# The router's product with its weights stationary, and the logits transposed back one step later, in a two-layer graph attention and mixture-of-experts kernel

## The chip, the cores and the metric

The kernel runs on one core of one Trainium2 chip. The core has five engines that run at the same time, each through its own list of instructions in order: TensorE (PE, matrix products and transposes, writing to PSUM), VectorE (DVE), ScalarE (ACT), GpSimd (POOL) and SyncE (SP, which here starts most of the transfers). They wait for each other through semaphores. The metric is the time of the whole kernel on the device in microseconds, the median over several runs.

## What is computed

The input is 128 graphs of 64 nodes with 256 features each, which makes 8192 rows (tokens). Two layers follow each other. Each adds to `x` first a graph attention of the normalised `x`, and then a mixture of experts of the normalised result. This change concerns the router of the mixture of experts, which picks two of eight experts for each row. Cut down to it:

```python
# layer 0
logits = tokens @ router_w.T                  # (8192, 256) @ (256, 8)
probs = softmax(logits); rw, re = top_k(probs, 2); rw = rw / rw.sum()
out = tokens + sum_e combine[:, e] * (gelu(tokens @ w1[e] + b1[e]) @ w2[e] + b2[e])
# layer 1
logits = x @ Wg + bg + bias                   # (8192, 256) @ (256, 8)
vals, idx = top_k(logits, 2); w = softmax(vals)
out = sum_e combine[:, e] * (relu(x @ W1[e] + b1[e]) @ W2[e] + b2[e])
```

All arithmetic is in 32-bit floating point.

## The kernel before

The rows are worked in blocks of 512 (four tiles of 128), 16 blocks in each layer, so 32 blocks. For each block there are two Python generators: `attend` (the attention) and `route` (layer norm, router, the places of the rows in the experts' lists). Each `yield` ends a step. Beside them, `Slots` works through the experts' lists in slots of 256 rows: `x` fetches the rows' transposes (px, L764; xT, L768), `h` makes the first product (ph, L846) with its activation (hT, L855), and `y` makes the second product (py, L877) and adds its bias (ys, L884). Layer 0 then scatters the rows by an indirect transfer (L893); layer 1 first weights them (L919) and adds them to the output (L922).

The order of the work is written out by hand: a loop over the blocks calls one step of one generator after the other. PE, DVE, ACT and SP run their instructions in exactly that order. POOL is not in that list, and its order is left to the framework's scheduler. For the block `t` that is being routed and the next one `n = t + 1` in attention, the part of the loop that matters here reads, before the change:

```python
a(n)          # pe (L309, L310), ee, the maximum (L325), the exponentials (L328)
r(t)          # pl (L419), lg, largest, the write of xb (L439)
if t + 2 != NB:
    a(t + 2)  # layer 1 only: eight DVE additions to xs (L267)
y()           # py (L877), ys (L884)
a(n)          # 1/sum (erc, L334) and its product with ee (L335)
(h if more else x)()
r(t)          # the second largest logit
a(n)          # pp: transposes of ee (L339), and their copies (L341, L342)
y()
```

The router's product itself has the transposed rows of the block as its stationary operand, and 8 columns of weights stream through: `pl[:, t, :]` (128 rows by 8 logits) is made by two products for each of the four tiles. DVE copies `pl` to `lg` (L428, or L430 and L431 with the biases in layer 1), and `largest` finds the largest logit, its place and its one-hot row (L372 to L383). The first three blocks run through chains that are written out beforehand, in which the steps of several blocks alternate; `(r, 0)] * 10` is the number of steps of such a chain.

PSUM tiles of the router share a ring of two buffers (tag `r`): two for the transposes of the rows (pt), one for pl, one for pn (L476). Tiles of one tag in SBUF share a ring too: tag `ex` has three buffers, and each block of the attention uses two.

Of the kernel before, what the change touches and what calls it, by code (L numbers as in the profile page):

```python
# [8 lines left out]
F32 = mybir.dt.float32  # L9
# [7 lines left out]
P = 128  # L17
NG = 64
D = 256
KD = D // P  # L20
E = 8
TT = 4
TB = TT * P
# [12 lines left out]
def adj_ffn_kernel(  # L36
# [34 lines left out]
    nc = tc.nc  # L71
# [19 lines left out]
    work = ctx.enter_context(tc.tile_pool(name="work", bufs=3))  # L91
    small = ctx.enter_context(tc.tile_pool(name="small", bufs=2))
    slot = ctx.enter_context(tc.tile_pool(name="slot", bufs=2))
    ps_c = ctx.enter_context(tc.tile_pool(name="ps_c", bufs=2, space=bass.MemoryType.PSUM))
# [25 lines left out]
    ident = const.tile([P, P], F32, name="ident")  # L120
# [5 lines left out]
    for g in range(2):  # L126
        r = slice(g * NG, (g + 1) * NG)
# [10 lines left out]
    start = const.tile([P, E], F32, name="start")  # L138
# [48 lines left out]
    rw = [const.tile([P, KD, E], F32, name=f"rw{l}") for l in range(2)]  # L187
# [57 lines left out]
    def transposed(src, tag, ptag, name, both):  # L245

        xt = work.tile([P, KD, TB], F32, tag=tag, name=f"xt_{name}", bufs=2)
        for k in range(KD):
            pt = ps_c.tile([P, TB], F32, tag=ptag, name=f"pt_{name}_{k}")
            for t in range(TT):  # L250
                nc.tensor.transpose(
                    pt[:, t * P : (t + 1) * P], src[:, t, k * P : (k + 1) * P], ident
                )
            if k % 2 == 0 and not both:
                nc.vector.tensor_copy(xt[:, k, :], pt)  # L255
            else:
                nc.scalar.copy(xt[:, k, :], pt)
        return xt
# [136 lines left out]
    def unordered(group, ins, keep=()):  # L395

        tc.declare_no_dep(
            ins.ins, group=group, keep=[i.ins for i in keep], reason="different rows"
        )
        tc.add_to_no_dep_group(group, ins.ins)  # L400

    def route(l, b, blk):

        name = f"r{l}_{b}"
# [8 lines left out]
        yield  # L413
        tT = transposed(tn, "tT", "r", name, l == 0 and b < FIRST)
        yield
        pl = ps_c.tile([P, TT, E], F32, tag="r", name=f"pl_{name}")
        for t in range(TT):
            for k in range(KD):
                nc.tensor.matmul(  # L419
                    pl[:, t, :],  # L420
                    lhsT=tT[:, k, t * P : (t + 1) * P],
                    rhs=rw[l][:, k, :],
                    start=(k == 0),
                    stop=(k == KD - 1),
                )
        lg = small.tile([P, TT, E], F32, tag="lg", name=f"lg_{name}")
        if l == 0:
            nc.vector.tensor_copy(lg, pl)  # L428
# [27 lines left out]
        r = slice(b * TT, (b + 1) * TT)  # L456
# [232 lines left out]
    class Slots:  # L689
# [139 lines left out]
        def h(self):  # L829
            k = self.nh  # L830
            self.weighted()
            if k == self.nx or k == self.ny + 2:
                return
            self.nh += 1
            sl = self.all[k]
            l = sl["l"]
            wc, xT = sl["wc"], sl["xT"]
            hT = slot.tile([P, HC[l], SL], F32, tag="hT", name=f"hT_s{k}")
            for f in range(0, HC[l], 2):
                ph = ps_s.tile([P, 2, SL], F32, tag="ph", name=f"ph_s{k}_{f}", bufs=2)  # L840
                cols = [slice(r.start * P, r.stop * P) for _, r in sl["of"]]
                for j in range(2):
                    for w, r in zip(wc, cols):
                        for c in range(KD):
                            o = c * HC[l] * P + (f + j) * P
                            nc.tensor.matmul(  # L846
                                ph[:, j, r],
                                lhsT=w[:, o : o + P],
                                rhs=xT[:, c, r],
                                start=(c == 0),  # L850
                                stop=(c == KD - 1),
                            )
                for j in range(2):
                    for w, r in zip(wc, cols):
                        nc.scalar.activation(  # L855
                            hT[:, f + j, r], ph[:, j, r], AF.Gelu if l == 0 else AF.Relu,
                            bias=w[:, OB1[l] + f + j : OB1[l] + f + j + 1],
                        )
            sl["hT"] = hT
            if l == 1 and sl["rest"]:  # L860
                self.spare(k)

        def y(self):
            k = self.ny
            self.weighted()
            if k == self.nh:
                return
            self.ny += 1
            sl = self.all[k]
            l = sl["l"]  # L870
            wc, hT = sl["wc"], sl["hT"]
            py = ps_s.tile([P, ST, D], F32, tag="py", name=f"py_s{k}")
            ys = slot.tile([P, ST, D], F32, tag="ys", name=f"ys_s{k}", bufs=4)
            for w, (_, r) in zip(wc, sl["of"]):
                for t in range(r.start, r.stop):
                    for f in range(HC[l]):
                        nc.tensor.matmul(  # L877
                            py[:, t, :],
                            lhsT=hT[:, f, t * P : (t + 1) * P],
                            rhs=w[:, O2[l] + f * D : O2[l] + (f + 1) * D],  # L880
                            start=(f == 0),
                            stop=(f == HC[l] - 1),
                        )
                nc.vector.tensor_tensor(  # L884
                    ys[:, r, :],
                    py[:, r, :],
                    w[:, OB2[l] : OB1[l]].unsqueeze(1).to_broadcast([P, r.stop - r.start, D]),
                    ALU.add,
                )
            sl["ys"] = ys  # L890
            for t in range(sl["st"]):
                if l == 0:
                    ins = nc.gpsimd.indirect_dma_start(  # L893
                        out=res[sl["part"]],
                        out_offset=self.row(sl, t),
                        in_=ys[:, t, :],
                        in_offset=None,
                        bounds_check=2 * N - 1,
                        oob_is_err=False,
                    )  # L900
                    unordered(f"res{sl['part']}", ins)
            if l == 1:
                self.ready = k
            self.ahead()
# [59 lines left out]
    def there(i):  # L964
        return 0 <= i < len(blks) and blks[i]

    def load(i, first=None):
        if there(i):
            k = blks[i]
            if k["l"]:  # L970
                assert all(s["l"] or s["part"] != part(k["b"]) for s in slots.all[slots.ny :])
            k["in"] = load_block(k["l"], k["b"], first)
            k["a"] = attend(k["l"], k["b"], k)

    def a(i, n=1):
        if there(i):
            for _ in range(n):
                next(blks[i]["a"], None)

    def r(i, n=1):  # L980
        if there(i):
            k = blks[i]
            if "r" not in k:
                k["r"] = route(k["l"], k["b"], k)
            for _ in range(n):
                next(k["r"], None)
# [15 lines left out]
    place = counted("place", [P, ST], [[P, ST]], 0, 1)  # L1002
    att = lambda b: [(a, b)] * 9 + [(a, b, 2), (a, b)]
    chains = [
        (0, att(0)[3:] + [(r, 0)] * 10),
        (1, att(1)[2:] + [(r, 1)] * 10),
        (2, att(2) + [(r, 2)] * 9),
        (8, att(3) + [(r, 3)] * 2),
        (12, [(a, 4)] * 3),
    ]  # L1010
# [28 lines left out]
    for t in range(FIRST, len(blks)):  # L1039
        n = t + 1  # L1040
        more = slots.nf - slots.ny > SB or len(slots.all) - slots.ny > SB
        if t + 3 != NB:
            load(t + 3)
        a(n)
        h()
        x()
        a(n)
        r(t - 1)
        a(n)
        h()  # L1050
        r(t)
        slots.fetch()
        if more:
            x()
        a(n)
        r(t)
        if t + 2 != NB:
            a(t + 2)
        y()
        a(n)  # L1060
        (h if more else x)()
        r(t)
        a(n)
        y()
        a(t + 2, 1 + (t + 2 == NB))
        if more:
            x()
        a(n)
        r(t)
        h()  # L1070
        a(n)
        if more:
            y()
        x()
        a(n)
        h()
        r(n)
        y()
        a(t + 2)
        r(t)  # L1080
        r(t)
        y()
        slots.fetch()
        x()
        r(n)
        r(t)
        if t + 3 == NB:
            load(t + 3)
# [57 lines left out]
```

## Time and profile before

| | before |
|---|---|
| median of 3 runs | 1437.01 us (1436.83 to 1442.47) |
| the profiled execution, its own time | 1675.06 us |
| span of the profile, first to last instruction | 1673.3 us |
| mean granted clock of TensorE | 0.882 of full |
| L419, the router's product, PE | 512 records, 81.8 us busy |
| L877 and L846, the experts' products, PE | 425.6 and 402.1 us busy |

The profile is one execution, taken by the hardware profiler, and it took longer than the runs without it. An engine's busy time is the time in which it had an instruction at work; the two rows of products are pipelined, so their records overlap, and the distance from one start to the next says more than the length of one. A product in 32-bit floating point appears as two records (two passes). In brackets a line of a timeline gives the idle time of the engine just before an instruction, and what ended it.

### The profile page before, as it was taken

The page shows a single profiled execution, that of the slowest core. Times are in us where ns is not written, and L with a number is a line of the kernel's source. Part 1 is how long each engine was busy: PE and PEld are TensorE (multiplying, and loading weights), DVE is VectorE, ACT ScalarE, POOL GpSimd, SP SyncE. Part 2 cuts the span into 40 slices and gives each one's busy share as a digit, 9 for nine tenths or more (in the row PEclk, how much of TensorE's full clock was granted, in tenths as well). Part 3 has the DMA queues.
Part 4 walks back from the last instruction along what each step waited for, and adds up shares of the span by engine and source line. Part 5 has one row for each costly group of instructions (what it writes and reads, how often), then busy time and mean ns, then how long its engine had stood idle before and what let it go on. Part 6 is the DMA issues. An engine that isn't in the chain of part 4 may idle for free. (4 is left out here: it accounts for less than half of the span.)

```text
span 1673.3 us, 22326 instructions
## 1 busy us (share of the span) xinstructions
PE 1305.4 (78%) x6240; PEld 1100.9 (66%) x6240; DVE 875.1 (52%) x3390; ACT 647.5 (39%) x1550; POOL 743.9 (44%) x729
## 2 busy tenths in 40 slices
PE   7657777777777667766768888988888988869994
PEld 5546665655665556555657777877777777658883
DVE  4555755574455566745565555655555654442331
ACT  5534444444433434333333434333344434223331
POOL 3164444444445543334442455444455444544324
PEclk9668988998888898788789999988889888989997
DMA  6535555575565654656765768666777656677873
GB/s 194 143 124 176 197 167 168 167 219 167 167 184 189 228 186 152 204 171 198 219 219 156 218 194 234 197 169 193 208 215 213 172 134 185 169 218 223 238 211 65
DMA packets 262829, 311.69 MB, mean 186 GB/s; under 512 B 40615, under 2 KB 219950, under 8 KB 262704
## 3 DMA queue, kind: packets, MB, share of 16 engines
q1 hardware_dynamic: 219552, 225.02, 43.7%
q0 software_dynamic: 43152, 85.24, 19.1%
q8 instruction: 50, 0.82, 0.2%
q14 instruction: 75, 0.61, 0.1%
HBM read 212.25 MB, written 99.75 MB: 186 GB/s over the span
## 5 line engine op out<-in xcount | busy, mean ns | idle before, releaser
L846 PE MATMUL ph_s<-xT_s,wc_s 128*128 128x256 f32 (+1 forms) x1760 | 402.1, 380 | 57.3 <-DVE xT_s L768 22.8
L877 PE MATMUL py_s<-wc_s,hT_s 128*128 128x256 f32 x1648 | 425.6, 411 | 21.8 <-issue 14.0
L846 PEld LDWEIGHTS ph_s<-xT_s,wc_s 128*128 128x128 f32 x1760 | 327.0, 198 | 116.3 <-DVE xT_s L768 29.9
L877 PEld LDWEIGHTS py_s<-wc_s,hT_s 128*128 128x128 f32 x1648 | 331.7, 207 | 75.9 <-issue 16.6
L922 POOL DMA_INDIRECT out_dram<-ys_s,to_s x135 | 212.8, 1576 | 366.7 <-ACT ys_s L919 215.7
L499 POOL DMA_INDIRECT lists<-tn_r,ix_r x256 | 249.5, 975 | 102.9 <-issue 71.9
L855 ACT ACTIVATE hT_s<-ph_s,wc_s 128x256 f32<-128x256 f32 (+1 forms) x440 | 175.8, 457 | 278.5 <-issue 117.2
L290 PE MATMUL pw_g<-gw,xt_g 128*128 128x258 f32 x512 | 157.6, 459 | 134.0 <-ACT wh_g L297 74.0
L893 POOL DMA_INDIRECT res<-ys_s,to_s x142 | 146.2, 1029 | 259.7 <-DVE erc_g L334 177.9
L290 PEld LDWEIGHTS pw_g<-gw,xt_g 128*128 128x128 f32 x512 | 109.5, 228 | 169.5 <-ACT wh_g L297 83.3
L768 DVE COPY xT_s<-px_s 128x512 f32<-128x512 f32 (+1 forms) x140 | 95.5, 682 | 204.4 <-remote 89.4
L884 DVE TENSOR_TENSOR ys_s<-py_s,wc_s 128x512 f32<-128x512 f32 (+1 forms) x149 | 97.4, 654 | 188.6 <-PE py_s L877 180.7
L419 PE MATMUL pl_r<-rw,xt_r 128*128 128x8 f32 x512 | 81.8, 295 | 45.4 <-DVE xt_r L255 40.9
L419 PEld LDWEIGHTS pl_r<-rw,xt_r 128*128 128x128 f32 x512 | 82.1, 246 | 51.7 <-DVE xt_r L255 45.2
L297 ACT COPY wh_g<-pw_g 128x258 f32<-128x258 f32 x128 | 47.0, 375 | 162.4 <-remote 82.0
L919 ACT ACTIVATE ys_s<-ys_s,cf_s 128x256 f32<-128x256 f32 x135 | 61.4, 500 | 105.7 <-DVE ys_s L884 105.4
L240 ACT ACTIVATE tn_r<-xb_g,nb_r,rs_r 128x256 f32<-128x256 f32 x128 | 66.5, 590 | 86.3 <-DVE nb_r L238 55.5
L240 ACT ACTIVATE xn_g<-xs,nb_g,rs_g 128x256 f32<-128x256 f32 x128 | 66.4, 590 | 66.3 <-DVE nb_g L238 66.3
L764 PE MATMUL px_s<-ident,xg_s 128*128 128x128 f32 x554 | 85.7, 278 | 0.2 <-DMA xg_s<-lists 0.2
L764 PEld LDWEIGHTS px_s<-ident,xg_s 128*128 128x128 f32 x554 | 70.7, 146 | 13.0 <-issue 1.0
L348 PE MATMUL po_g<-wh_g,pT_bd 128*128 128x256 f32 x256 | 70.8, 425 | 8.5 <-ACT pT_bd L342 7.0
L342 ACT COPY pT_bd<-pp_g 64x256 f32<-64x256 f32 x32 | 11.7, 365 | 163.7 <-DVE pT_bd L341 160.6
(503 smaller groups left out, 1583.8 us busy)
## 6 DMA issues: line engine op xcount, KB each, us to landing
wc_s<-in_w_dram SPq DMA_DIRECT2D x142, 512.0 KB
wc_s<-in_w_dram SPq DMA_DIRECT2D x156, 256.0 KB
xg_s<-lists SPq DMA_DIRECT2D x64, 260.0 KB
xg_s<-lists SPq DMA_DIRECT2D x64, 258.0 KB
yb<-res SPq DMA_DIRECT2D x16, 1024.0 KB
wc_s<-bcat SPq DMA_DIRECT2D x78, 129.0 KB
wc_s<-bcat SPq DMA_DIRECT2D x71, 130.0 KB
xs<-in_x_dram SPq DMA_DIRECT2D x16, 512.0 KB
```

What stands on the lines that cost most here:

```text
L240: nc.scalar.activation(outs(t), xb[:, t, :], AF.Identity, bias=nb[:, t : t + 1], scale=rs[:, t : t + 1])
L290: nc.tensor.matmul(pw, lhsT=xt[:, k, t * P : (t + 1) * P], rhs=gw[l][:, k, :], start=(k == 0), stop=(k == KD - 1),)
L419: nc.tensor.matmul(pl[:, t, :], lhsT=tT[:, k, t * P : (t + 1) * P], rhs=rw[l][:, k, :], start=(k == 0), stop=(k == KD - 1),)
L499: ins = nc.gpsimd.indirect_dma_start(out=lists[l], out_offset=bass.IndirectOffsetOnAxis(ap=ix[:, k, t : t + 1], axis=0), in_=tn[:, t, 0 : ...
L764: nc.tensor.transpose(px[:, c, t * P : (t + 1) * P], xg[:, t, c * P : (c + 1) * P], ident)
L768: nc.vector.tensor_copy(xT[:, :, 0 : st * P], px[:, :, 0 : st * P])
L846: nc.tensor.matmul(ph[:, j, r], lhsT=w[:, o : o + P], rhs=xT[:, c, r], start=(c == 0), stop=(c == KD - 1),)
L855: nc.scalar.activation(hT[:, f + j, r], ph[:, j, r], AF.Gelu if l == 0 else AF.Relu, bias=w[:, OB1[l] + f + j : OB1[l] + f + j + 1],)
L877: nc.tensor.matmul(py[:, t, :], lhsT=hT[:, f, t * P : (t + 1) * P], rhs=w[:, O2[l] + f * D : O2[l] + (f + 1) * D], start=(f == 0), stop=(f ...
L884: nc.vector.tensor_tensor(ys[:, r, :], py[:, r, :], w[:, OB2[l] : OB1[l]].unsqueeze(1).to_broadcast([P, r.stop - r.start, D]), ALU.add,)
L893: ins = nc.gpsimd.indirect_dma_start(out=res[sl["part"]], out_offset=self.row(sl, t), in_=ys[:, t, :], in_offset=None, bounds_check=2 * N - 1,
L922: ins = nc.gpsimd.indirect_dma_start(out=out, out_offset=self.row(sl, t), in_=ys[:, t, :], in_offset=None, compute_op=ALU.add,)
```

## The change

The two operands of the router's product change sides. The weights (128 by 8) become the stationary operand, and the 512 rows of the block stream through in one product for each half of the features: 2 products instead of 8. The result `pq` stands the other way round, 8 logits by 512 rows. ACT copies it to SBUF (`lT`, in a buffer of tag `ex`), and there the step ends. A new step transposes it back on PE, four transposes of 8 by 128, into `pl` as it was. From there on nothing is different.

In the loop, the first of the two steps stands where the old one stood, and the second stands behind `y()`. So in the order of the engines `py` and `ys` come ahead of the transposes and of `lg` and `largest`, and so do the additions to `xs` of layer 1. The chains of the first blocks get one step more.

```diff
         tT = transposed(tn, "tT", "r", name, l == 0 and b < FIRST)
         yield
+
+        pq = ps_c.tile([E, TB], F32, tag="r", name=f"pq_{name}")
+        for k in range(KD):
+            nc.tensor.matmul(
+                pq, lhsT=rw[l][:, k, :], rhs=tT[:, k, :], start=(k == 0), stop=(k == KD - 1)
+            )
+        lT = work.tile([E, TB], F32, tag="ex", name=f"lT_{name}")
+        nc.scalar.copy(lT, pq)
+        yield
         pl = ps_c.tile([P, TT, E], F32, tag="r", name=f"pl_{name}")
         for t in range(TT):
-            for k in range(KD):
-                nc.tensor.matmul(
-                    pl[:, t, :],
-                    lhsT=tT[:, k, t * P : (t + 1) * P],
-                    rhs=rw[l][:, k, :],
-                    start=(k == 0),
-                    stop=(k == KD - 1),
-                )
+            nc.tensor.transpose(pl[:, t, :], lT[:, t * P : (t + 1) * P], ident[0:E, 0:E])
...
-        (0, att(0)[3:] + [(r, 0)] * 10),
-        (1, att(1)[2:] + [(r, 1)] * 10),
-        (2, att(2) + [(r, 2)] * 9),
+        (0, att(0)[3:] + [(r, 0)] * 11),
+        (1, att(1)[2:] + [(r, 1)] * 11),
+        (2, att(2) + [(r, 2)] * 10),
...
             a(t + 2)
         y()
+        r(t)
         a(n)
         (h if more else x)()
         r(t)
```

## The prediction

> **What bounds the kernel now.** I read the engine shares, the groups, the chain that ended last, the waits, and then the timelines of four engines around the router's product. The shares:
>
> ```profile
> PE 1305.4 (78%) x6240; PEld 1100.9 (66%) x6240; DVE 875.1 (52%) x3390; ACT 647.5 (39%) x1550; POOL 743.9 (44%) x729
> PEclk9668988998888898788789999988889888989997
> ```
>
> PE leads, but it is not full and its clock is often below full. The chain that ended last covers the tail only (13% of the span, scatters and the last products, which the change does not touch), so the answer has to come from one block's stretch.
>
> ```profile
> L419 PE MATMUL pl_r<-rw,xt_r 128*128 128x8 f32 x512 | 81.8, 295 | 45.4 <-DVE xt_r L255 40.9
> ```
>
> 512 records are 32 blocks of 8 products with two passes each. Now layer 0, block 7, PE first (start, length, engine, line):
>
> ```profile
> 275.13 0.59 PE L310 MATMUL pe_g<-wh_g,ident 128*128 128x256 f32 x2
> 275.56 1.85 PE L419 MATMUL pl_r<-rw,xt_r 128*128 128x8 f32 x16
> 277.27 1.97 PE L877 MATMUL py_s<-wc_s,hT_s 128*128 128x256 f32 x8
> 279.08 0.60 PE L764 MATMUL px_s<-ident,xg_s 128*128 128x128 f32 x4
> 280.66 0.60 PE L339 MATMUL pp_g<-ident,ee_g 128*64 128x128 f32 x4 [0.98 <-DVE ee_g L335]
> ```
>
> From start to start, pl takes 1.71 us (16 passes, 107 ns each). PE then stands 0.98 us before pp, for DVE's ee. VectorE in the same stretch:
>
> ```profile
> 276.22 0.42 DVE L325 TENSOR_REDUCE emx_g<-ee_g 128x4 f32<-128x256 f32 x1
> 277.45 0.19 DVE L428 COPY lg_r<-pl_r 128x32 f32<-128x32 f32 x1 [0.81 <-PE pl_r L419]
> ...
> 278.57 0.19 DVE L383 TENSOR_TENSOR oh_r_7a<-eq_r_7a,mo_r_7a 128x32 f32<-128x32 f32 x1
> 279.28 0.69 DVE L884 TENSOR_TENSOR ys_s<-py_s,wc_s 128x512 f32<-128x512 f32 x1 [0.52 <-PE py_s L877]
> 279.89 0.17 DVE L334 RECIPROCAL erc_g<-esm_g 128x4 f32<-128x4 f32 x1
> 280.09 0.42 DVE L335 TENSOR_TENSOR ee_g<-ee_g,erc_g 128x256 f32<-128x256 f32 x1
> ```
>
> The chain lg to oh (six operations, 1.33 us) runs while PE does py: it costs nothing now, for it fits between two idle stretches (0.81 and 0.52 us). From ys at 279.28 DVE has no idle over 0.1 us until 287.2, and PE waits for it. So in layer 0 DVE after py sets the pace. ScalarE there:
>
> ```profile
> 278.05 0.19 ACT L328 ACTIVATION_READ_ACCUMULATOR ee_g<-ee_g,emx_g 128x1 f32 x1
> 278.14 2.06 ACT L435 ACTIVATE xb_g<-xb_g,nb_r,rs_r 128x256 f32<-128x256 f32 x4
> ```
>
> Layer 1 differs: DVE has eight more operations (xs, 3.75 us) between oh and ys, and no gap:
>
> ```profile
> 735.78 0.42 DVE L325 TENSOR_REDUCE emx_g<-ee_g 128x4 f32<-128x256 f32 x1
> 736.14 0.19 DVE L430 TENSOR_TENSOR lg_r<-pl_r,gb 128x32 f32<-128x32 f32 x1
> ...
> 737.59 3.75 DVE L267 SCALAR_TENSOR_TENSOR xs<-yb,cs,xs 128x256 f32<-128x256 f32 x8
> 741.25 0.69 DVE L884 TENSOR_TENSOR ys_s<-py_s,wc_s 128x512 f32<-128x512 f32 x1
> 742.06 0.43 DVE L335 TENSOR_TENSOR ee_g<-ee_g,erc_g 128x256 f32<-128x256 f32 x1
> ```
> ```profile
> 742.63 0.60 PE L339 MATMUL pp_g<-ident,ee_g 128*64 128x128 f32 x4 [2.98 <-DVE l_r L445]
> ```
>
> PE idles 2.98 us there; DVE alone sets that stretch.
>
> **The two times.** The profiled execution took 1675.06 us (span 1673.3), the median is 1437.01: 238 us less. The trace has waits of 3 to 6 us whose releaser it cannot name ("remote", as 6.03 us before xT at 530); I take much of the difference to be these. I therefore read prices from stretches free of them and add them to 1437.
>
> [...] half-rate pieces come in multiples of 3.41 us, 395 us of the span in all. [...]
>
> **Part by part, for one block.**
> 1. Removed: the eight products of pl, 1.71 us of PE.
> 2. Added in their place: pq, 2 products of two passes over 512 columns. A 256-column pass takes 0.216 us from start to start (py: 8 passes in 1.73 us before px's load), so 4 passes of twice that are 1.73 us. Passes grow with the columns (258: 0.218), and fewer stationary columns make none shorter (pp with 64 and px with 128 both stand 0.109 apart); so a gain is excluded as far as the trace goes, and at half clock both forms double. On PE: 0.
> 3. Added on ACT: lT, a copy of 8x512 out of PSUM. Nearest row, xt_r at 128x512: 0.59 us. It stands behind the four exponentials (end 278.24) and is done at about 278.8, before py's end at 279.08, so it is hidden by py. Were that cover gone, PE would wait up to 0.6 us. Behind it on ACT is xb, 0.6 us later; pT, next on ACT, comes only at 283.13, so nothing waits.
> 4. Added on PE behind py: four transposes of 8x128. [...] I take 0.44, the price of px's four. DVE meanwhile does ys (0.61 us), so lg can start at once after ys[...].
> 5. Moved: lg to oh goes from ahead of ys to behind it, ahead of erc and ee. In layer 0 the hole that it filled stays empty (2.6 us idle where there were 1.33), and its 1.33 us now stand between py's end and pp. With px between py and pp (blocks 4 to 10) ee, pp, the next py, pT and po all come 1.33 us later. With ph there (11 to 15) PE has 1.3 us more cover, but pp is still 1.07 us late, and the second ys, for which DVE had waited 0.86 us, 1.1 us. What is late next is the chain ys, bn_stats, xT, ph and so to the next block; I find no later wait in the block with slack. So 7 x 1.33 + 5 x 1.1 = 14.8 us.
> 6. Layer 1: xs moves ahead of lg, fills the hole and covers py, then ys, then lg. DVE's sum before ee is the same, and PE's transposes lie in its 2.98 us wait. 16 x 0. Cover gone (PE at half clock, py ending after xs, as at 1308.31 in the trace): up to 1.5 us each.
> 7. Blocks 0 to 3 have no product of a slot between pq and its transposes: copy, transposes and two handovers lie open, 1.2 us each at most. Block 3 pays it, of the three interleaved start chains I count 2 us in all: 3.2 us.
> 8. Queues: SP's order is unchanged, row for row. On POOL six rows change places with a neighbour (the write of xb goes behind a scatter); POOL is 44% busy and stood 10 us idle here (0). lT shares the buffers of ex, three of them, with three uses per block; each is free an iteration earlier (0). The logits' PSUM ring gets five tiles per block instead of four, each released by a copy that PE already waits for (0).
>
> Sum: 14.8 + 0 + 3.2 = 18.0 us; against the profiled time 1675 to 1693, against the median 1437.0 + 18.0 = 1455. Half a per cent, 7 us, is about what a measurement of this kernel can tell from no change.
>
> **The rivals.**
> - Faster, by the clock. While pl runs, hardly a column streams, and that counts as idle: the window before the drop at 1044.5 us has pl in 40% of it, and columns in 3%. pq streams all the time. [...] For it: five of the 42 drops in the trace follow a window with pl in it. Against it: only two of the five would have been lifted over the 35% above which no drop is seen. [...]
> - Slower still: the cover of point 6 is gone, or PE's longer hole before pp (about 2.3 us instead of 1.0 in layer 0) itself lowers the clock. For it: the steady blocks of layer 1 in the trace have half clock exactly there. 1455 + 16 x 1.5 = 1479.
> - No change: the delay of layer 0 is absorbed by a transfer that comes last anyway. For it: DMA is at 87% share at 506 to 512 us. Against it: PE's own list of waits names DVE and ACT, no transfer. 1437 to 1442.
> - That the change does not do what it says: excluded by the built order, which has pq, py, pl in that order in the loop.
>
> **How the numbers follow.** Likeliest 0.45 (its own range 1448 to 1464), slower still 0.18, no change 0.13, faster 0.24. The predicted time is 1455. The range 1430 to 1482 leaves out most of the gain by the clock and the far end of the slow case. Faster 0.24, same 0.13, slower 0.63.
>
> **What would show it.** Right: pq at 1.7 us per block and pl about 0.44; PE's wait before pp on ee grown from 1.0 to about 2.3 us in layer 0, and about 2.5 us instead of 3.0 in layer 1; DVE idle some 2.6 us before ys in layer 0; lT ended before py. Wrong: less half clock than 395 us; pq well under 1.7 us; ee as early after py as before.

## The result, and the profile after

The changed kernel takes 1454.47 us (median of 4 runs, 1452.77 to 1458.89) against 1436.92 us for the kernel before on the same chip (4 runs, 1436.69 to 1442.47). The ratio is 1.0116, with a 95% interval of 1.0087 to 1.0144: slower by 17.5 us, where 18.0 had been predicted.

The profiled execution after took 1458.89 us (span 1457.1), close to the runs. That of before, which the prediction was read from, had taken 1675.06 us, so the two pages must not be laid side by side. The kernel before was therefore profiled once more (first experiment, 1437.71 us, span 1435.9), and all comparisons below use that second profile, called "before, second profile". From the page of the changed kernel, the engines, the granted clock and the router's product:

```profile
PE 1233.9 (85%) x5984; PEld 992.1 (68%) x5984; DVE 873.1 (60%) x3390; ACT 662.8 (45%) x1582; POOL 741.7 (51%) x729
PEclk9867899999999999899999999999999999999997
L419 PE MATMUL pq_r<-xt_r,rw 128*8 128x512 f32 x128 | 64.3, 627 | 0.3 <-DVE xt_r L255 0.3
```

512 short records have become 128 longer ones. Two more names are needed in what follows: pT is the copy of pp in SBUF, of which DVE and ACT make one half each, and po (L348) is the product that PE makes from pT. In one block of layer 0 (block 6, with px between py and pp) the timeline of PE reads, in the changed kernel (start, length, engine, line; in brackets the idle time ahead, and what ended it):

```profile
221.55 0.59 PE L310 MATMUL pe_g<-wh_g,ident 128*128 128x256 f32 x2
222.08 1.89 PE L419 MATMUL pq_r<-xt_r,rw 128*8 128x512 f32 x4
223.89 1.99 PE L879 MATMUL py_s<-wc_s,hT_s 128*128 128x256 f32 x8
225.82 0.41 PE L427 MATMUL pl_r<-ident,lT_r 8*128 8x8 f32 x4
226.16 0.66 PE L766 MATMUL px_s<-ident,xg_s 128*128 128x128 f32 x4
228.43 0.63 PE L339 MATMUL pp_g<-ident,ee_g 128*64 128x128 f32 x4 [1.62 <-DVE ee_g L335]
```

and in before, second profile:

```profile
211.90 0.59 PE L310 MATMUL pe_g<-wh_g,ident 128*128 128x256 f32 x2
212.33 1.85 PE L419 MATMUL pl_r<-rw,xt_r 128*128 128x8 f32 x16
214.03 1.97 PE L877 MATMUL py_s<-wc_s,hT_s 128*128 128x256 f32 x8
215.84 0.60 PE L764 MATMUL px_s<-ident,xg_s 128*128 128x128 f32 x4
217.43 0.60 PE L339 MATMUL pp_g<-ident,ee_g 128*64 128x128 f32 x4 [0.98 <-DVE ee_g L335]
```

From the second pe (L310) to pp it was 5.53 us and is 6.88: 1.35 more. DVE shows why. In before, second profile, it reads in that block (ys starts when py has ended, at 216.01)

```profile
214.22 0.19 DVE L428 COPY lg_r<-pl_r 128x32 f32<-128x32 f32 x1 [0.80 <-PE pl_r L419]
...
215.52 0.19 DVE L383 TENSOR_TENSOR oh_r_6a<-eq_r_6a,mo_r_6a 128x32 f32<-128x32 f32 x1
216.05 0.69 DVE L884 TENSOR_TENSOR ys_s<-py_s,wc_s 128x512 f32<-128x512 f32 x1 [0.33 <-DMA lists<-tn_r,ix_r]
216.66 0.17 DVE L334 RECIPROCAL erc_g<-esm_g 128x4 f32<-128x4 f32 x1
216.86 0.43 DVE L335 TENSOR_TENSOR ee_g<-ee_g,erc_g 128x256 f32<-128x256 f32 x1
```

and in the changed kernel

```profile
222.64 0.42 DVE L325 TENSOR_REDUCE emx_g<-ee_g 128x4 f32<-128x256 f32 x1
225.92 0.69 DVE L886 TENSOR_TENSOR ys_s<-py_s,wc_s 128x512 f32<-128x512 f32 x1 [2.86 <-PE py_s L879]
226.53 0.18 DVE L430 COPY lg_r<-pl_r 128x32 f32<-128x32 f32 x1
...
227.64 0.19 DVE L383 TENSOR_TENSOR oh_r_6a<-eq_r_6a,mo_r_6a 128x32 f32<-128x32 f32 x1
227.75 0.17 DVE L334 RECIPROCAL erc_g<-esm_g 128x4 f32<-128x4 f32 x1
227.95 0.42 DVE L335 TENSOR_TENSOR ee_g<-ee_g,erc_g 128x256 f32<-128x256 f32 x1
```

The hole ahead of ys now has nothing in it (2.86 us idle), and lg to oh stands between ys and ee. In layer 1 (block 7 there) PE of the changed kernel reads

```profile
885.35 1.88 PE L419 MATMUL pq_r<-xt_r,rw 128*8 128x512 f32 x4
887.16 3.72 PE L879 MATMUL py_s<-wc_s,hT_s 128*128 128x256 f32 x16
890.82 0.41 PE L427 MATMUL pl_r<-ident,lT_r 8*128 8x8 f32 x4
891.16 0.66 PE L766 MATMUL px_s<-ident,xg_s 128*128 128x128 f32 x4
893.66 0.63 PE L339 MATMUL pp_g<-ident,ee_g 128*64 128x128 f32 x4 [1.84 <-DVE ee_g L335]
```

and the same block of before, second profile:

```profile
862.05 1.85 PE L419 MATMUL pl_r<-rw,xt_r 128*128 128x8 f32 x16
863.75 3.70 PE L877 MATMUL py_s<-wc_s,hT_s 128*128 128x256 f32 x16
867.29 0.60 PE L764 MATMUL px_s<-ident,xg_s 128*128 128x128 f32 x4
870.57 0.60 PE L339 MATMUL pp_g<-ident,ee_g 128*64 128x128 f32 x4 [2.68 <-DVE ee_g L335]
```

Here the added transposes have gone into PE's wait (2.68 became 1.84), and a steady block takes 44.7 us in both.

**Where the time lies.** The start of each attention block's pe in the trace is a mark whose place in the block no edit changes; what the iteration that routes block t loses is in full at the pe of block t+2. Against before, second profile, each kernel has gained or lost in each stretch (us; one profiled execution each, blocks by the routed one; the last column is the difference of the medians of the runs). The last mark is the pe of block 31, so the last two routed blocks and what follows them are in no column; there the form alone loses another 5.5 us and the place alone 6.1, and each of the others at most 1.3:

| kernel | blocks 0 to 3 | layer 0, 4 to 10 | layer 0, 11 to 15 | layer 1 | sum | medians |
|---|---|---|---|---|---|---|
| the change | +4.7 | +10.2 | +7.1 | -1.0 | +21.0 | +17.5 |
| in layer 0 alone | +4.6 | +11.0 | +3.7 | +0.6 | +19.9 | +18.2 |
| in layer 1 alone | 0.0 | 0.0 | -0.4 | -1.7 | -2.1 | -5.4 |
| ee first | +3.7 | +7.8 | +3.6 | -13.6 | +1.5 | -0.5 |
| hole filled | +1.3 | +7.6 | +2.2 | -4.7 | +6.4 | +7.3 |
| form alone | +4.0 | +10.8 | +9.0 | +27.7 | +51.5 | +53.4 |
| place alone | +6.0 | +5.1 | +1.9 | +15.5 | +28.4 | +30.0 |
| pT early, new form | -1.3 | -1.9 | -0.6 | -20.7 | -24.5 | -28.7 |
| pT early, old form | +0.6 | -1.0 | -3.5 | -20.8 | -24.7 | -28.1 |
| pT early, new form, and ee ahead of ys | -1.9 | -4.8 | -1.0 | -25.3 | -33.0 | -34.1 |

The clock records show stretches of half clock; one of them, called a piece here, lasts 3.41 us or a multiple of it, but for the last of a profile (19.8 us in the first). A single one of 3.41 us makes a block 1.7 us longer (46.34 us against 44.65 in the late blocks of layer 1 with the change), so single cells are good to some 3 us; the sums stay within 4.2 us of the medians.

### The profile page after: what moved, and what is told of

Its sections match the earlier page's. It is cut to its first block, busy times and chain, and to the rows that moved or that the text cites. A ratio compares the mean times of both kernels' runs of the same rounds, so it can differ in the third digit from the quotient of the medians.

```text
span 1457.1 us, 21821 instructions
## 1 busy us (share of the span) xinstructions
PE 1233.9 (85%) x5984; PEld 992.1 (68%) x5984; DVE 873.1 (60%) x3390; ACT 662.8 (45%) x1582; POOL 741.7 (51%) x729
## 5 line engine op out<-in xcount | busy, mean ns | idle before, releaser
L848 PE MATMUL ph_s<-xT_s,wc_s 128*128 128x256 f32 (+1 forms) x1760 | 394.4, 375 | 57.5 <-DVE xT_s L770 38.5
L879 PE MATMUL py_s<-wc_s,hT_s 128*128 128x256 f32 x1648 | 397.7, 391 | 22.3 <-issue 14.0
L848 PEld LDWEIGHTS ph_s<-xT_s,wc_s 128*128 128x128 f32 x1760 | 318.1, 193 | 112.9 <-DVE xT_s L770 52.6
L879 PEld LDWEIGHTS py_s<-wc_s,hT_s 128*128 128x128 f32 x1648 | 311.5, 195 | 93.0 <-issue 38.7
L290 PE MATMUL pw_g<-gw,xt_g 128*128 128x258 f32 x512 | 125.8, 396 | 19.1 <-DVE xt_g L255 16.0
L290 PEld LDWEIGHTS pw_g<-gw,xt_g 128*128 128x128 f32 x512 | 96.7, 197 | 39.6 <-issue 16.4
L766 PEld LDWEIGHTS px_s<-ident,xg_s 128*128 128x128 f32 x554 | 68.4, 144 | 10.8 <-issue 0.4
L348 PE MATMUL po_g<-wh_g,pT_bd 128*128 128x256 f32 x256 | 65.9, 403 | 8.7 <-ACT pT_bd L342 7.4
L279 POOL TENSOR_SCALAR cap_g<-adj 128x256 f32<-128x256 int32 x32 | 35.2, 1100 | 69.9 <-DMA adj<-in_adj_dram 45.2
L342 ACT COPY pT_bd<-pp_g 64x256 f32<-64x256 f32 x32 | 11.7, 364 | 123.9 <-DVE pT_bd L341 123.8
L419 PE MATMUL pq_r<-xt_r,rw 128*8 128x512 f32 x128 | 64.3, 627 | 0.3 <-DVE xt_r L255 0.3
```

Source lines behind the costliest of these rows:

```text
L290: nc.tensor.matmul(pw, lhsT=xt[:, k, t * P : (t + 1) * P], rhs=gw[l][:, k, :], start=(k == 0), stop=(k == KD - 1),)
L348: nc.tensor.matmul(po[h][:, j, :], lhsT=pT[:, 2 * h + j, :], rhs=wh[:, 2 * h + j, 0:D], start=True, stop=True,)
L766: nc.tensor.transpose(px[:, c, t * P : (t + 1) * P], xg[:, t, c * P : (c + 1) * P], ident)
L848: nc.tensor.matmul(ph[:, j, r], lhsT=w[:, o : o + P], rhs=xT[:, c, r], start=(c == 0), stop=(c == KD - 1),)
L879: nc.tensor.matmul(py[:, t, :], lhsT=hT[:, f, t * P : (t + 1) * P], rhs=w[:, O2[l] + f * D : O2[l] + (f + 1) * D], start=(f == 0), stop=(f ...
```

## The experiments

Every kernel here does the whole work. Each ratio is to the kernel before on the same chip, with its 95% interval.

**The kernel before once more.** No edit.

> The kernel before, unchanged, profiled once more. The profile shown of it took 1675 us where its runs take 1437, and had PE waits of 3 to 6 us that nothing in the trace releases. Theory (those waits belong to that one execution, not to the kernel): the profiled time comes within 1 per cent of 1437, half-clock time falls well under 395 us towards the 148 us of the changed kernel, and layer 0 still shows 5.3 us from the start of pe's last product to pp's start. Rival (the kernel before really has these waits, and the changed one does not): a profiled time near 1675 again with the waits in the same blocks.

The profiled execution took 1437.71 us, and ten runs 1438.30 in the median (ratio 0.9993, 0.9977 to 1.0010). The page of before, second profile:

```profile
PE 1215.5 (85%) x6240; PEld 1041.5 (73%) x6240; DVE 875.1 (61%) x3390; ACT 646.9 (45%) x1550; POOL 742.4 (52%) x729
PEclk9767999989999998999999999999999999989997
```

The first profile had a busier PE (1305.4 us) for the same instructions. Summed over the clock records, the half clock is 146 us in this profile and 148 in that of the changed kernel; 395 in the first. So the extra 238 us, and most of the half clock, belonged to that one execution. The prices of the prediction survive, since they were read from undisturbed blocks: pe's last product to pp's start is 5.31 us here too.

**Layer 0 alone, layer 1 alone.** The new form, its extra step and its place only where `l == 0`, then only where `l == 1`:

```diff
+        if l == 0:
             pq = ps_c.tile([E, TB], F32, tag="r", name=f"pq_{name}")
...
+        else:
+            pl = ps_c.tile([P, TT, E], F32, tag="r", name=f"pl_{name}")
...
-        r(t)
+        if blks[t]["l"] == 0:
+            r(t)
         a(n)
```

The `else` holds the eight old products; the second kernel has 1 in place of 0, and the old number of steps in the first chains.

> The change in layer 0 alone; layer 1 keeps the eight products with 8 columns at their old place. Theory (the 18 us lie in layer 0, where DVE's chain lg to oh has left its hole ahead of ys): 14.8 + 3.2 = +18 us, about 1455, as the full change. Rival (the form itself costs, the same in every block): half of it, about 1446. Rival (layer 1 carries it): 1437 to 1440.

1457.92 us (6 runs), ratio 1.0124 (1.0103 to 1.0145): the whole loss, +18.2.

> The change in layer 1 alone; layer 0 is as before. Theory (in layer 1 the additions to xs fill the hole and DVE's sum ahead of ee is the same): 0, so 1437, within 3 us. Rival (the form itself costs, the same in every block): about 1446. Rival (the cover of py is gone at half clock): up to +24, 1461.

1434.41 us (6 runs), ratio 0.9952 (0.9937 to 0.9966): no loss; 5 us faster, a little beyond the 3 that the theory allowed. The profile of this run accounts for 2 of the 5 (one half-clock piece less, and blocks that are 0.1 us shorter); the rest is open. The loss is in layer 0, and it is not a price per block that the form costs everywhere. The two halves add to 12.8 us where the whole change costs 17.5; the difference of 4.7 is within the intervals of the three runs taken together.

**ee first.** The two steps behind py change places:

```diff
         y()
-        r(t)
         a(n)
+        r(t)
```

> The changed kernel with the two steps behind py exchanged: 1/sum and ee come ahead of the logits' transposes, lg and largest. pp then no longer waits for lg to oh. Theory (in layer 0 DVE's sum behind py sets the block, so it matters little which of its parts comes first): 1450 to 1456, as the full change; pp is back at 5.3 us from pe, but what follows pp on DVE is late all the same. Rival (the whole cost is that pp waits for lg to oh): back to 1437 to 1441.

1439.24 us (21 runs), ratio 0.9987 (0.9974 to 0.9999). The total is the rival's number, but the table shows that the rival is not what happened: layer 0 keeps most of its loss (11.4 us in blocks 4 to 15, and steady blocks take 32.2 us, as with the change, against 30.7 before), and layer 1 gains 13.6. PE in block 6 of layer 0 of this kernel:

```profile
224.47 0.63 PE L339 MATMUL pp_g<-ident,ee_g 128*64 128x128 f32 x4 [0.40 <-DVE ee_g L335]
224.93 1.89 PE L879 MATMUL py_s<-wc_s,hT_s 128*128 128x256 f32 x8
228.66 1.99 PE L348 MATMUL po_g<-wh_g,pT_bd 128*128 128x256 f32 x8 [1.84 <-ACT pT_bd L342]
```

pp is early again, but po now waits for the copies pT, which stand on DVE behind lg to oh, xT and the second largest logit (ACT's half of pT, which the line names, itself waits for DVE's half). The wait has moved, not gone: from pe (the second product) to po it is 9.86 us, as with the change, and 8.41 before. In layer 1, DVE has slack behind pp, and po's wait is only 0.60 us where pp's had been 1.84: a steady block takes 44.1 us instead of 44.7, and in blocks 6 to 14 of layer 1 no half clock is left (3 pieces before).

**The hole filled.** The statistics of block t+2 ahead of ys, in layer 0:

```diff
         if t + 2 != NB:
-            a(t + 2)
+            a(t + 2, 1 + (t + 2 < NB))
         y()
...
-        a(t + 2, 1 + (t + 2 == NB))
+        if t + 2 >= NB:
+            a(t + 2, 1 + (t + 2 == NB))
```

> The changed kernel, with the layer-norm statistics of block t+2 (eight operations and two more, 2.3 us of DVE) moved ahead of the second product in layer 0, into the hole of 2.9 us that DVE now has there; layer 1 as changed. Theory A (the prediction's: DVE's whole sum behind py sets a block of layer 0, the statistics in it): they leave that sum, at least 1.2 us of each of 12 blocks, so 1440 or less. Theory B (DVE's sum counts only up to the copies pT, from which po, ph, px on PE set the pace; xT waits 0.5 us for px in the trace): the statistics stand behind pT, so their going gives nothing, 1452 to 1456.

1446.79 us (14 runs), ratio 1.0047 (1.0030 to 1.0064): between the two. The two kinds of block of layer 0 answer differently. Where px stands between py and pp, nothing changes: blocks 5 to 8 lose 5.6 us together, with the change 5.8. That is theory B. Where ph stands there (block 13), the changed kernel had

```profile
480.39 1.99 PE L348 MATMUL po_g<-wh_g,pT_bd 128*128 128x256 f32 x8
483.83 1.99 PE L848 MATMUL ph_s<-xT_s,wc_s 128*128 128x256 f32 x8 [1.45 <-DVE xT_s L770]
```

and this one

```profile
470.17 1.89 PE L348 MATMUL po_g<-wh_g,pT_bd 128*128 128x256 f32 x8
471.90 1.89 PE L848 MATMUL ph_s<-xT_s,wc_s 128*128 128x256 f32 x8
```

since there xT stands on DVE behind the statistics. Blocks 11 to 13 go from +5.0 to -1.1 us (+2.5 in the run with layer 0 alone). That is theory A. The rest of the gain lies in the first blocks and in layer 1, and its cause stays open.

**The form alone.** No `yield` behind the copy, and no second `r(t)`, so that pq, lT and the transposes stand where pl stood:

```diff
         nc.scalar.copy(lT, pq)
-        yield
...
         y()
-        r(t)
         a(n)
```

> The new form alone: pq, its copy lT, and the transposes back in one step at the old place, ahead of py, lg and largest too. Theory (lT stands behind the four exponentials on ACT, and without py as cover PE waits for it): in layer 0 PE stands some 1.3 us and py and ys come 1.8 us later, 12 times 1.8 = 22; in layer 1 DVE gets lg 2.4 us later and stands, 16 times 2.4 = 38; start 3: about 1503. Rival (only PE's own added work counts, about 0.5 us in 28 blocks): 1455. Rival (the copy is hidden as well here): 1440.

1492.88 us (4 runs), ratio 1.0370 (1.0348 to 1.0393). PE's list of waits for this kernel begins

```profile
PE pl_r L426 <- ACT lT_r L423: 46.9, 32, 2.0
```

46.9 us in 32 blocks: 1.21 us in block 6 of layer 0, 1.95 in a late block of layer 1 (at 903.70). So py is the cover of the copy, and the form without the move costs 53 us; layer 1 has 28 of them up to the last mark and 33 to the end, where 38 were expected.

**The place alone.** The eight old products, moved with lg and largest behind py:

```diff
         yield
-        pq = ps_c.tile([E, TB], F32, tag="r", name=f"pq_{name}")
...
-        nc.scalar.copy(lT, pq)
         yield
...
-            nc.tensor.transpose(pl[:, t, :], lT[:, t * P : (t + 1) * P], ident[0:E, 0:E])
+            for k in range(KD):
+                nc.tensor.matmul(
+                    pl[:, t, :],
+                    lhsT=tT[:, k, t * P : (t + 1) * P],
+                    rhs=rw[l][:, k, :],
...
```

> The place alone: the eight products with 8 columns as before, moved with lg and largest behind py; no pq, no copy, no transposes back. In layer 0 py and ys come 1.7 us earlier, lg starts when pl is done, 4.1 us from pe, and lg to oh (1.3 us) lies ahead of ee again, so pp comes 0.7 us later than before instead of 1.35. Theory (what counts is how late lg to oh lets ee and the copies pT): 12 times 0.7 = 8, about 1448; layer 1 0. Rival (the form costs, not the place): 1440. Rival (the place alone is the whole cost): 1455.

1470.68 us (5 runs), ratio 1.0208 (1.0186 to 1.0230): far above all three. Layer 0 did what was expected: pp 0.52 us later, and blocks 4 to 15 cost 7.0 us. Layer 1, expected at 0, cost 15.5 up to the last mark. PE in block 8 of layer 1 of this kernel:

```profile
925.77 3.62 PE L878 MATMUL py_s<-wc_s,hT_s 128*128 128x256 f32 x16
929.22 1.85 PE L420 MATMUL pl_r<-rw,xt_r 128*128 128x8 f32 x16
930.93 0.63 PE L765 MATMUL px_s<-ident,xg_s 128*128 128x128 f32 x4
934.25 1.03 PE L339 MATMUL pp_g<-ident,ee_g 128*64 128x128 f32 x4 [2.69 <-DVE ee_g L335]
935.08 6.11 PE L878 MATMUL py_s<-wc_s,hT_s 128*128 128x256 f32 x16
```

The same py takes 3.62 us at 925.77 and 6.11 behind the hole: the clock was halved at 933.3 for 6.83 us. From the start of pl to pp, 5.0 us, PE streams little: pl has 8 columns in each pass, and only px (0.44 us) has more. In the changed kernel the stretch from py's end to pp is 2.8 us (890.82 to 893.66), and before it was 3.3 (867.29 to 870.57), because there pl lay on the other side of py. In nine blocks of layer 1, from the pe of block 6 to that of block 15, the half clock is 48 us here, 7 with the change and 10 before. From the kernel before this one differs only in the place of pl, lg and largest, so it is shown that this place, with the old products in it, brings the added half clock (48 us against 10). From the changed kernel it differs in the form, and with it in where most of the product stands: pq is ahead of py, and only the short transposes are behind it.

What PE did ahead of each drop can be read from its records. The starts of all 42 pieces of the first profile lie whole multiples of 3.41 us apart; they mark off windows of that length. In each window add up the time in which columns stream (0.84 ns for each column of a pass at full clock, from 0.43 us for 512). In the twelve profiles 258 windows at full clock were followed by half clock: none has columns streaming for more than 40% of it. Of the 4239 that kept full clock, after the first 13 us, none has less than 35%. In the first profile and in that of the changed kernel alone, 62 windows of the first kind have at most 36% and 689 of the second at least 35%. The windows ahead of the nine drops in those nine blocks here have 13 to 29%. If the time of pl counted in full, four of the nine would have 43 to 75%. So half clock followed although PE was at work on products with 8 columns for much of four of them. That a product with 512 columns in the same place would have kept the clock in these four is an estimate from the same numbers; no run has it there.

**pT early, in the new and in the old form.** Behind py: ee, then lg and largest, then pp with the copies pT, and only then the second largest logit; the statistics in the hole as above. The edits to the loop, beside those of the filled hole:

```diff
         y()
-        r(t)
         a(n)
+        r(t)
         (h if more else x)()
-        r(t)
         a(n)
+        r(t)
         y()
```

> The new form with another order behind py: ee first, then the transposes, lg and largest, then pp and its copies pT ahead of the second largest logit, and the statistics of block t+2 in DVE's hole ahead of ys in layer 0. Theory B (DVE up to the copies pT sets layer 0, and po's wait for pT in layer 1): in layer 0 po comes 1.7 us earlier than with ee first alone and xT 1.6, 12 times 1.6 = 19; in layer 1 po's wait of 0.6 goes, 16 times 0.6 = 10; from 1439 to about 1411. Rival (transfers or POOL take over as the limit, DMA's share being 78 to 87 per cent there): 1430 or more.

1410.79 us (5 runs), ratio 0.9793 (0.9768 to 0.9817). Theory B's number, but not stage by stage: against ee first, the table gives 13.9 us of the 19 in blocks 4 to 15 and 7.1 of the 10 in layer 1, and another 5.0 in the first blocks, for which the theory had no term. Steady blocks take 30.7 us in layer 0 (32.2 with the change) and 43.2 in layer 1 (44.7). This kernel beats both the changed one and the one before.

The second kernel has that order with the eight old products at their old place, and a step of its own for lg and largest:

```diff
...
-        lT = work.tile([E, TB], F32, tag="ex", name=f"lT_{name}")
-        nc.scalar.copy(lT, pq)
-        yield
         pl = ps_c.tile([P, TT, E], F32, tag="r", name=f"pl_{name}")
...
+                    stop=(k == KD - 1),
+                )
+        yield
         lg = small.tile([P, TT, E], F32, tag="lg", name=f"lg_{name}")
```

> The order of the run before this one, with the old form: eight products with 8 columns at the old place, and a step of its own for lg and largest behind ee. It tells the form by itself. In the trace the new form takes 0.21 us more from pe to py and its transposes 0.34 us more behind py. Theory (where DVE no longer sets the pace, PE's own work counts): 0.55 us less in some 20 to 28 blocks, 11 to 15 us under the run before this one, about 1398. Rival (the form is hidden wherever it stands): the same time as the run before this one, within 3 us. Rival (a product with 8 columns counts as idle for the clock): more half-clock time and a slower kernel than the run before this one.

1411.35 us (5 runs), ratio 0.9806 (0.9782 to 0.9829): the same time, so the first theory falls, and with this order the form makes no difference. In block 9 of layer 1 PE of the new form reads

```profile
944.96 0.63 PE L339 MATMUL pp_g<-ident,ee_g 128*64 128x128 f32 x4 [0.40 <-DVE ee_g L335]
```

and of the old form

```profile
944.75 0.60 PE L339 MATMUL pp_g<-ident,ee_g 128*64 128x128 f32 x4 [1.21 <-DVE lg_r L432]
```

What the old form saves on PE, PE waits ahead of pp. The half clock was 156 us against 123, as the rival by the clock has it, but the time is the same.

**ee ahead of ys.** One step more in the new form:

```diff
+        a(n)
         y()
-        a(n)
         r(t)
```

> The fastest order so far (ee first, pT early, statistics in the hole) with 1/sum and ee moved once more, ahead of ys, which takes 0.6 us of DVE. pp waits 0.4 us for ee in both layers there. Theory (this wait is still on the path of a block): it goes, 0.4 us in some 28 blocks, 1411 to about 1400. Rival (ys comes late instead and what waits for it takes the gain): 1408 to 1414.

1406.57 us (5 runs), ratio 0.9768 (0.9746 to 0.9789), between the two ranges. PE's wait ahead of pp for ee fell from 11.7 us in 22 waits to 1.3 in one, and steady blocks of layer 1 fell from 43.2 to 42.8 us, 0.4 as expected. The profiled executions differ by 9.7 us (1411.3 to 1401.6), the medians only by 4.2. It is the fastest kernel of the study.

## Why the prediction was right, step by step

**The two times.** Right: the delayed waits belonged to the profiled execution. What followed from it was not drawn to its end: most of the 395 us of half clock came from the same execution, and its use as a mark ("less half clock than 395 us") would have told a gain where there was none. Against 146 us of before, second profile, the 148 of the changed kernel are no change.

**Steps 1 and 2, pl against pq.** pl was 1.70 us. Its passes stand 0.112 us apart, not 0.107: the prediction divided by 16, but the second follows the first after only 0.03. The price of pl is the same. pq's four passes stand 0.43 us apart, 1.72 in all, as predicted; but PE stood 0.09 us both ahead of pq and behind it (0.53 us from pe to pq, 0.43 from pe to pl before). From pe to py it is 2.34 us instead of 2.13. The step "On PE: 0" is off by 0.21 us, and in layer 0 ys waits for py, so it counts in 12 blocks: 2.5 us. What causes the two gaps of 0.09 us no run shows. At half clock both forms double, as predicted: pl's passes stand 0.213 us apart there (medians, first profile) and pq's 0.853 (changed kernel).

**Step 3, lT.** Right: 0.56 us (predicted 0.59), from 224.56 to 225.12, py until 225.88. What it would cost uncovered was too low: not 0.6 us but 1.2 to 2.0, because the copy is also late behind the exponentials, as the form alone shows.

**Step 4, the transposes.** 0.09 us gap and 0.34 us to px: 0.43, predicted 0.44. That the number fits is luck: the transposes stand only 0.061 us apart where 0.109 had been taken, 0.25 us for four, and two gaps of 0.09 us, which the 0.44 left out, make up the rest. Each has 128 stationary columns, as pl's passes had, but its loads start 0.06 us apart where those of pl start 0.112. Whether the 8 rows or the kind of operation makes the difference is open.

**Step 5, layer 0.** Right in mechanism and nearly in size. ee ends 1.43 us later after the second pe than before (6.82 against 5.39 in block 6): 1.22 are lg to oh (226.53 to 227.75; the term was 1.33, and the prediction's own lines give 1.31), the rest is the 0.22 by which ys starts later, step 2's. Blocks 5 to 8 lose 1.45 us each. Blocks 4 to 10 cost 10.2 us (9.3), blocks 11 to 15 cost 7.1 (5.5). 14.8 with step 2's 2.5 is 17.3, and 17.2 were measured; that these agree so closely is luck, for in the run with layer 0 alone the same blocks cost 14.7, and pieces of half clock lie in them. What is late next was named as one chain for all blocks, "ys, bn_stats, xT, ph". That failed for blocks with px: filling the hole took the statistics out of the sum there, and nothing came of it. In those blocks the sum of DVE ends at the copies pT, and PE's po, ph and px follow: with pT early a steady block is back from 32.2 to 30.7 us, as before the change. With ph between py and pp (blocks 11 to 13) the chain is as written.

**Step 6, layer 1.** Right: 0, and PE's wait shortened (2.68 to 1.84 us; from 2.98 to about 2.5 was expected). But its reason was not complete. The place alone has the same sum on DVE and lost 15.5 us, with 48 us of half clock in the nine blocks. In the changed kernel the 512 columns stream ahead of py, only 0.34 us of transposes stand behind it, and the half clock there is 7 us. So the rival "by the clock" did not decide between before and after (10 and 7 us of half clock in the nine blocks), but what it builds on, half clock behind products with 8 columns, is what the move with the old form would have met. What a drop costs was the author's estimate in it: 4 of the 42 pieces in its own trace last one window of 3.41 us and the others longer, and 9 of 19 in before, second profile, last one window.

**Step 7, the start.** 3.2 us predicted, 4.7 measured up to the end of block 3. PE's list of waits of the changed kernel has the open copies:

```profile
PE pl_r L427 <- ACT lT_r L423: 2.9, 4, 1.1
```

2.9 us in four waits, of at most 1.1 us each (1.2 at most was estimated). The rest of the 4.7 is not explained; the hole filled, which starts in the same way, lost 1.3 in these blocks.

**Step 8, queues.** Nothing in the trace speaks against 0; it was not tried by itself.

**The rivals.** "Slower still" by a longer hole that lowers the clock did not come; the place alone is that case. Nor did the half clock of the steady blocks of layer 1 in the first profile lie in the hole before pp: in the block at 1293.86 it lasts from 1297.1 to 1307.4 us, over pl and py, and pp starts at 1309.71. "No change" by a transfer that comes last is excluded: with the same transfers, another order of the steps took the kernel from 17.5 us above the one before to 34.1 below it.

**The sum.** 18.0 us were predicted and 17.5 measured; in the profile it is 4.7 + 10.2 + 7.1 - 1.0 = 21.0. The mechanism of the prediction holds, in layer 0 with the correction for blocks with px. That its number comes within 0.5 us is partly luck: stage by stage it was off by 1.5, 0.9, 1.6 and 1.0 us, the runs of the changed kernel alone span 6 us, and step 2's 2.5 us were missing from it.

## What to carry to other kernels

A step that is moved out of another engine's idle time must be paid where it lands, even if the work itself costs the same: here 1.2 us of VectorE ahead of a product that PE waits for. Read the two halves of a change against each other: the form alone cost 53 us, the place alone 30, both 17.5, since each hides what the other would lay open. A total that matches a theory's number does not confirm it; split it by stage first ("ee first" came out at no change as a loss in one layer and a gain in the other).

## What the runs showed of the hardware

- Half clock follows a window in which few columns stream, even where products with 8 columns keep PE at work in it. Over all twelve profiles, after the first 13 us, a window of 3.41 us at full clock was always followed by half clock when columns streamed in less than 35% of it, and never when they streamed in more than 40%. With 1.7 us of such products beside a wait of 2.7 us, half clock came in nine late blocks of layer 1 out of nine; with the same products ahead of py and the same wait, in three of nine. In the first of these two kernels a block with one piece of 3.41 us takes 46.0 to 46.4 us and one with two 47.1 to 47.7; a block without any takes 44.7 with the change. The wait of 2.7 us is by itself shorter than a window of 3.41; the products with 8 columns fill the rest.
- One profiled execution of an unchanged kernel took 1675 us, another 1438. Such a profile still has good prices in its undisturbed blocks (pe's last product to pp's start is 5.31 us in both), but not its sums.
- A pass of 8 stationary columns and 512 streamed ones takes 0.43 us, twice that of 128 and 256 (0.216): at these lengths fewer stationary columns make no pass shorter. Transposes with 8 rows of data, which stream 8 columns, stand 0.061 us apart, against 0.109 for 128 rows and columns.
